# Late counts by prefix sums and minima, column forms with a second tensor, columns in a group's fifth block, and another order at start and end, in a one-core graph layer

## The chip, the cores and the metric

The kernel runs on one core of one Trainium2 chip. The metric is the device time of the kernel in microseconds (us); less is better. Engines are called PE (TensorE), DVE (VectorE), ACT (ScalarE), POOL (GpSimd) and SP (SyncE).

## The reference, cut to what matters

There are 50,000 nodes with 128 features and 1,650,000 edges, sorted by their target node. Every edge has a type, 0 or 1.

```python
m_data = X[src] @ W_data.T + b_data
m_ctrl = X[src] @ W_control.T + b_control
msg = where(edge_types == 0, m_data, m_ctrl)
agg = segment_sum(msg, dst, num_segments=50000)
out = relu(agg + X @ W_self.T + b_self)
return layernorm(x + out)
```

The weights are linear, so the kernel sums the source rows first, for each target node and type, and multiplies by the weights afterwards.

## The kernel before

**Blocks.** The edges are cut in order into 514 blocks (`NBLK`, numbers 0 to 513). A block's targets lie in a window of 112 nodes. A block holds `Q` = 2 steps of `R` = 12 chunks of 128 edges, so 24 chunks. POOL fetches the 128 source rows of a chunk (512 bytes each) by one indirect DMA, a *gather* (`gathers`, L536). Six gathers make a pass (`PASS`), a pass fills one buffer `y`, and there are ten buffers (`SLOTS`). PE multiplies each chunk's rows with a one-hot matrix of the chunk's target columns (128 x 120, both types side by side) and sums them in `acc` (`products`, L555). DVE builds the one-hot matrices of a whole block in one comparison (`onehot`, L467) and counts edges for the biases (`counts`, L475), two blocks ahead. `add` (L569) adds a step's sums to the block's.

**Single rows and fillers.** Besides its 24 chunks a block has 48 edges whose rows SP and ACT fetch one by one (`single_rows`, L510), and edges that fill the places which edges from a node to itself leave free in the chunks, since these are taken from the block's own rows. Such *fillers* come from a list per step with `F` = 46 places and `LATE` = 10 more for those that had to wait, `FX` = 56 in all. `spread(b)` (L347) is three small PE products that copy the list of block b to all partitions. `fill(b)` (L356 to L377) is DVE work: it finds which place takes which filler, writes the list `idx` of block b that the gathers read (L369) and the columns that `onehot` reads (L370). Blocks 0 and 513 are plain, without fillers; POOL needs no `fill` for them.

**Columns.** Ten blocks make a group (`GB`), 52 in all. `columns(g)` (L279 to L335) does for a whole group what can be done at once: the columns of its edges (`columns_of`, L240 to L243), checks (L248 to L251), the packed number of source and column (`packed`, L256 and L258), the list's three parts `v_f` (L296 to L302), the column numbers `cb` (L305 to L307), the rank of every free place (`rank` on PE, L284 and L286; `rk`, L311), and the number of waiting fillers `late`. That last is a chain: each of 20 steps is max(0, more + late of the step before), one `tensor_scalar` on a 128 x 1 column each (L323), as the group before left its last count.

**Order.** The order of all work is written out by hand, and each engine runs its instructions in that order. Before the loop stand the constants, the numbers of blocks (L207 to L223: windows, registers' values and shifts, needed by `window`, `positions` and the final checks), then the lines that make block 0, 1 and 2. The loop over b puts, in turn: spreads of the lists to be made, `add` of the block before, `onehot` and `counts` of block b+2, and four passes, between which stand `fill`, `layer(b-1)` (L586 to L590, the weights), `moments` (L596 to L603), `columns`, `store` (L618, L621: the normalised rows of a pair of blocks) and `store_rows` (L626, an output DMA per block on SP). Lists are made up to five blocks ahead (`RAHEAD`), two per block until then. `columns(g+1)` stands after the third pass of a group's second block:

```python
if q == 2 and i == 1 and g + 1 < GROUPS:
    columns(g + 1)
```

`find_bad` (L631 to L659) is a check of the input's form that chooses, at the end, whether the general version must run; it does not run here. It stands before the last block.

Of the kernel before, what the change touches and what calls it, by code (L numbers as in the profile page):

```python
# [12 lines left out]
F32 = mybir.dt.float32  # L13
BF16 = mybir.dt.bfloat16
# [9 lines left out]
N = 50000  # L24
# [57 lines left out]
GS = GB * Q  # L82
SPAN = 8
# [14 lines left out]
def straight(ctx, tc, c, x, x_t, edges_t, edges_f, src_x, dst_first, first_p, out):  # L98
# [62 lines left out]
    row_of = keep.tile([GB, GB], BF16, name="row_of")  # L161
    nc.vector.tensor_copy(row_of, c["ident"][:GB, :GB])
# [41 lines left out]
    nc.vector.tensor_tensor(begin_p, begin_p, base_p, op=ALU.add)  # L204
    wide = keep.tile([1, WG, SPAN], F32, name="wide")
    bases_f = keep.tile([1, WG * SPAN], F32, name="bases_f")
    nc.vector.memset(bases_f, float(N - B))  # L207
    nc.vector.tensor_copy(bases_f[:, :NBLK], base[0:1, :NBLK, 0])
    first_of_span = bases_f.rearrange("o (w s) -> o w s", s=SPAN)
    nc.vector.tensor_scalar(wide, first_of_span[:, :, 0:1].to_broadcast([1, WG, SPAN]), float(N - WIDE), None, op0=ALU.min)  # L210
    within = keep.tile([1, WG, SPAN], F32, name="within")
    nc.vector.tensor_tensor(within, first_of_span, wide, op=ALU.subtract)
    at_i = keep.tile([1, WG * SPAN, 4], I32, name="at_i")
    nc.vector.tensor_copy(at_i[:, :NBLK, :Q], begin[0:1, :NBLK, :])
    nc.vector.tensor_scalar(at_i[:, :, 3], within.rearrange("o w s -> o (w s)"), 0.0, float(WIDE - B), op0=ALU.max, op1=ALU.min)
    nc.vector.tensor_tensor(begin, begin, base.to_broadcast([P, BL, Q]), op=ALU.add)
    base_i = keep.tile([1, WG, 2 * SPAN], I32, name="base_i")
    nc.vector.tensor_scalar(base_i[:, :, 0], wide[:, :, 0], 4.0, None, op0=ALU.mult)
    nc.vector.tensor_scalar(base_i[:, :, 1:1 + SPAN], first_of_span, float(ROW), None, op0=ALU.mult)
    shift = keep.tile([1, NBLK], F32, name="shift")  # L220
    nc.vector.memset(shift, 0.0)
    nc.vector.tensor_tensor(shift[:, 1:], base[0:1, 1:NBLK, 0], base[0:1, :NBLK - 1, 0], op=ALU.subtract)
    nc.vector.tensor_scalar(at_i[:, :NBLK, 2], shift, 0.0, float(B), op0=ALU.max, op1=ALU.min)  # L223


# [10 lines left out]
    def columns_of(d, t, first, name):  # L236

        rel = eds.tile(list(d.shape), F32, name="rel" + name, bufs=1)
# [5 lines left out]
        return col, rel  # L244
# [8 lines left out]
    def packed(src, col):  # L253

        lim = eds.tile(list(col.shape), F32, name="lim", bufs=1)
        nc.vector.tensor_scalar(lim, col, 0.0, float(COLS - 1), op0=ALU.max, op1=ALU.min)  # L256
        v = eds.tile(list(col.shape), F32, name="v")
        nc.vector.scalar_tensor_tensor(v, src, float(COLS), lim, op0=ALU.mult, op1=ALU.add)  # L258
        return v

    def columns(g):
# [27 lines left out]
        col, rel = columns_of(a["d"], a["t"], first_of, "")  # L289
        check(a["d"], rel, [stats[:, 0, m, g:g + 1] for m in range(2)], "")  # L290
        col_f, rel_f = columns_of(a["df"], a["tf"], first_of_f, "_f")
# [5 lines left out]
        with nc.allow_low_precision(reason="whole numbers below 256 times a power of two"):  # L297
            nc.vector.tensor_scalar(v_f[:, 0, :], col_f, 0.0, float(COLS - 1), op0=ALU.max, op1=ALU.min)
            lo = eds.tile([GB, Q * FX], F32, name="lo", bufs=1)
            nc.vector.scalar_tensor_tensor(lo, hi, -float(COLS), a["sf"], op0=ALU.mult, op1=ALU.add)  # L300
# [14 lines left out]
        more = eds.tile([P, GS], F32, name="more", bufs=1)  # L315
        nc.vector.tensor_scalar(more, rank[:, :, R], -1.0, float(F), op0=ALU.mult, op1=ALU.add)
        late = eds.tile([P, GS + 1], F32, name="late")
        if g == 0:
            nc.vector.memset(late, 0.0)
        else:  # L320
            nc.vector.tensor_copy(late[:, 0:1], late_g[g - 1][:, GS:])
        for k in range(at, n):
            nc.vector.tensor_scalar(late[:, k + 1:k + 2], more[:, k:k + 1], late[:, k:k + 1], 0.0,  # L323
                                    op0=ALU.add, op1=ALU.max)
# [5 lines left out]
        if n < GS and g > 0:  # L330
            nc.vector.memset(late[:, n + 1:], 0.0)
# [8 lines left out]
    def spread(b):  # L340

        if plain(b):
            return
        g, i = divmod(b, GB)
        vf = lists[b % 2][:, :Q * FX]
        for m in range(3):
            nc.tensor.matmul(vf, row_of[:, i:i + 1].to_broadcast([GB, P]), vp_g[g][:, m, :], start=m == 0, stop=m == 2)  # L347
# [74 lines left out]
    def passes_of(b):  # L422

        for p in range(C // PASS):
            q = p * PASS // R
            yield q, [k for k in chunks_of(b, q) if k // PASS == p]
# [155 lines left out]
    def layer(b):  # L582
        a = sums[b % RING]
# [3 lines left out]
        nc.tensor.matmul(po, xT, c["wselfT"], start=True, stop=False)  # L587
        nc.tensor.matmul(po, a[0:3, 2, :B], bias, start=False, stop=False)  # L588
        for t in range(2):
            nc.tensor.matmul(po, a[:, t, :B], c["wmsgT"][:, t * D:(t + 1) * D], start=False, stop=t == 1)  # L590
        pos[b] = both

    def moments(b):
# [6 lines left out]
        if b % 2 == 0:  # L600
            mvs[b // 2] = stp.tile([B, 2, 2], F32, name="mv")
        mv = mvs[b // 2][:, b % 2, :]
        nc.vector.bn_aggr(mv, st)  # L603
        hs[b] = h

    def pair(b):

        return range(b // 2 * 2, b + 1) if b % 2 == 1 or b == NBLK - 1 else ()

    def root(bs):  # L610
        sd = stp.tile([B, 2], F32, name="sd")
        nc.scalar.activation(sd[:, :len(bs)], mvs[bs[0] // 2][:, :len(bs), 1], AF.Sqrt, bias=c["eps"][:B, :])
        sds[bs[0] // 2] = sd

    def store(bs):
        mv = mvs.pop(bs[0] // 2)
        rstd = stp.tile([B, 2], F32, name="rstd")
        nc.vector.reciprocal(rstd[:, :len(bs)], sds.pop(bs[0] // 2)[:, :len(bs)])  # L618
# [41 lines left out]

    for b in range(1, AHEAD + 1):
        offsets(b)
    columns(0)
    window(0)
    spread(1)
    fill(1)
# [3 lines left out]
    onehot(0)  # L670
    counts(0)
# [10 lines left out]
    for b in range(NBLK + 1):  # L682
        if b == NBLK - 1:
            find_bad()
# [5 lines left out]
        due, fresh = fresh, range(made + 1, min(b + RAHEAD, made + 2, NBLK - 1) + 1)  # L690
# [5 lines left out]
        if b < NBLK:  # L696
            begin_sums(b)
# [5 lines left out]
        for q, (step, ks) in enumerate(passes_of(b)):  # L703
# [21 lines left out]
            if q == 2 and i == 1 and g + 1 < GROUPS:  # L725
                columns(g + 1)
# [9 lines left out]
    store(pair(NBLK - 1))  # L736
    for b in (*ready, *pair(NBLK - 1)):
        store_rows(b)
# [338 lines left out]
```

## Time and profile before

| what | value |
|---|---|
| median of 3 runs | 17994.12 us (17983.56 to 17994.94) |
| profiled execution, its own time | 18008.86 us |
| its span | 18006.8 us |
| granted TensorE clock | 0.540 |
| POOL busy | 11686.9 us (65%) |
| DVE busy | 12374.8 us (69%) |
| PE busy | 8608.7 us (48%) |

In rows of groups the columns are: line, engine, operation, written tile <- read tiles, shapes, count; then busy time and the mean ns of one; then idle time of the engine just before them, and what ended it. Rows of waits give engine, tile and line, the releaser, the total, the number of times and the longest. Rows of the timeline give start, duration, engine, line, operation, and in brackets the idle time before with its releaser. "remote" is a releaser that the profile could not name, "issue" is time in which nothing visible was waited for.

### The profile page before, as it was taken

How to read it: one execution, taken by the hardware profiler on the slowest of the kernel's cores; microseconds unless marked ns; L12 is line 12 of the kernel's file. 1: busy time of each engine (PE TensorE's matmuls, PEld its weight loads, DVE VectorE, ACT ScalarE, POOL GpSimd, SP SyncE). 2: the span in 40 equal slices, each digit the busy share in tenths (PEclk: the TensorE clock that was granted, in tenths of full speed). 3: DMA queues.
4: the chain of work that ended last, by engine and by line, in shares of the span. 5: the costliest groups of instructions: out<-in, count | busy, mean ns of one | idle time of the engine just before them, and what ended most of it. 6: DMA issues, size and time to landing. Idle time of an engine off the chain costs nothing.

```text
span 18006.8 us, 165600 instructions
## 1 busy us (share of the span) xinstructions
PE 8608.7 (48%) x37659; PEld 7345.2 (41%) x37660; DVE 12374.8 (69%) x15212; ACT 79.2 (0%) x263; POOL 11686.9 (65%) x12341
## 2 busy tenths in 40 slices
PE   3444444444444444444444444444444444444444
PEld 3344443444344444444444444444444444444444
DVE  7676676676666666666766766676676676667665
ACT  0000000000000000000000000000000000000000
POOL 6666666666666666666666666666666666666666
PEclk6555555555555555555555555555555555555555
DMA  1111111111111111111111111111111111111111
GB/s 52 51 50 51 52 50 51 52 50 51 50 52 51 50 52 50 51 51 51 51 50 52 51 50 51 51 51 51 51 51 50 51 52 50 51 52 50 51 50 48
DMA packets 529272, 913.91 MB, mean 51 GB/s; under 512 B 232762, under 2 KB 315875, under 8 KB 528274
## 3 DMA queue, kind: packets, MB, share of 16 engines
q0 software_dynamic: 394592, 808.89, 15.7%
q1 hardware_dynamic: 108668, 87.80, 1.7%
q10 hardware_dynamic: 25014, 6.54, 0.2%
q8 instruction: 306, 5.01, 0.1%
q14 instruction: 692, 5.67, 0.1%
HBM read 872.82 MB, written 29.47 MB: 50 GB/s over the span
## 4 chain that ended last, share of the span: by engine, by line
DVE 51%; another core or an unknown queue 28%; issue 13%; PE 7%; DVEq 0%; ACTq 0%; ACT 0%
DVE cnt L475 14%; DVE oh L467 8%; PE acc L555 5%; DVE m L358 4%; DVE v_new L365 4%; DVE new L361 4%; DVE old L374 4%; DVE sums L569 2%; DVE late L323 1%; DVE z L392 1%; DVE h L597 1%; DVE st L599 1%; DVE xT L461 1%; DVE h L596 1%
## 5 line engine op out<-in xcount | busy, mean ns | idle before, releaser
L536 POOL DMA_INDIRECT y<-in_x,idx x12312 | 11667.4, 948 | 6272.6 <-issue 3435.2
L555 PEld LDWEIGHTS acc<-oh,y 128*128 128x128 f32 x24662 | 5375.0, 315 | 8665.3 <-issue 8100.0
L555 PE MATMUL acc<-oh,y 128*128 128x120 f32 x24662 | 6002.7, 413 | 3679.8 <-issue 3675.4
L569 DVE TENSOR_TENSOR sums<-acc,sums 128x180 f32 x1028 | 350.0, 340 | 4142.8 <-remote 3960.0
L475 DVE TENSOR_REDUCE cnt<-oh 128x240 bf16<-128x3120 f32 x514 | 3008.2, 5852 | 17.9
L384 PE MATMUL small<-ones_b,by 128*112 128x1 bf16 x512 | 83.5, 164 | 4632.6 <-issue 3934.5
L467 DVE TENSOR_TENSOR oh<-col,small 128x3120 f32<-128x3120 f32 x514 | 1740.8, 3387 | 117.3 <-remote 95.1
L377 DVE TENSOR_REDUCE by<-old 128x112 bf16<-128x1456 f32 x512 | 1427.3, 2788 | 17.4
L358 DVE TENSOR_TENSOR m<-rk,small 128x1456 f32<-128x1456 f32 x512 | 855.7, 1671 | 17.4
L361 DVE TENSOR_TENSOR new<-m,small 128x1456 f32<-128x1456 f32 x512 | 855.2, 1670 | 17.5
L365 DVE TENSOR_REDUCE v_new<-new 128x26 f32<-128x1456 f32 x512 | 855.0, 1670 | 17.5
L374 DVE TENSOR_TENSOR old<-m,small 128x1456 f32<-128x1456 f32 x512 | 852.5, 1665 | 0.0
L561 PE MATMUL acc<-oh,yx 24*128 24x120 f32 x2048 | 758.6, 466 | 61.6 <-issue 61.6
L590 PE MATMUL po<-wmsgT,sums 128*112 128x128 f32 x2056 | 612.8, 453 | 5.5 <-issue 5.5
L561 PEld LDWEIGHTS acc<-oh,yx 24*128 24x128 f32 x2048 | 486.9, 292 | 293.0 <-issue 281.7
L596 DVE COPY h<-po 112x128 f32<-112x128 f32 x514 | 144.8, 282 | 537.1 <-remote 451.3
L590 PEld LDWEIGHTS po<-wmsgT,sums 128*112 128x112 f32 x2056 | 448.4, 297 | 130.7 <-issue 130.0
L347 PE MATMUL small<-v_f,row_of 10*128 10x112 bf16 x1536 | 218.2, 272 | 563.8 <-DVE at L391 168.6
L588 PE MATMUL po<-bias,sums 3*112 3x128 f32 x1028 | 391.5, 482 | 0.2 <-DVE sums L569 0.2
L347 PEld LDWEIGHTS <-row_of 10*128 10x128 bf16 x1536 | 121.7, 112 | 599.5 <-issue 562.2
L587 PE MATMUL po<-wselfT,xT 128*112 128x128 f32 x1028 | 324.9, 420 | 0.0
L564 PE MATMUL acc<-cnt,to_row 128*128 128x60 bf16 x2056 | 281.2, 227 | 13.8 <-issue 13.7
(141 smaller groups left out, 4709.2 us busy)
## 6 DMA issues: line engine op xcount, KB each, us to landing
y<-in_x,idx POOLq DMA_INDIRECT x12312
yx<-in_x SPq DMA_DIRECT2D x12288, 0.5 KB
yx<-in_x ACTq DMA_DIRECT2D x12288, 0.5 KB
xw<-in_x_t SPq DMA_DIRECT2D x65, 448.0 KB
out<-o SPq DMA_DIRECT2D x514, 56.0 KB
sdt<-in_edges_t SPq DMA_DIRECT2D x52, 390.0 KB
one_g<-in_src_x SPq DMA_DIRECT2D x52, 1.9 KB
sdt_f<-in_edges_f SPq DMA_DIRECT2D x52, 13.1 KB
```

Source lines behind the costliest of these rows:

```text
L358: nc.vector.tensor_tensor(m, rk_g[g][:, i, :, None].to_broadcast([P, C1, FX]), rank_no_ps[:, None, :].to_broadcast([P, C1, FX]), op=ALU.is ...
L361: nc.vector.tensor_tensor(new.rearrange("p (q r) f -> p q r f", r=R1), m.rearrange("p (q r) f -> p q r f", r=R1), vf.rearrange("p (q f) -> ...
L365: nc.vector.tensor_reduce(v, new, AX.X, ALU.add)
L374: nc.vector.tensor_tensor(old, m, cb[:, :, None].to_broadcast([P, C1, FX]), op=ALU.mult)
L377: nc.vector.tensor_reduce(by, old.rearrange("p (q r) f -> p q f r", r=R1), AX.X, ALU.add)
L467: nc.vector.tensor_tensor(oh, col_g[g][:, i, :, None].to_broadcast([P, C1, 2 * W]), num_ps[:, None, :].to_broadcast([P, C1, 2 * W]), op=AL ...
L475: nc.vector.tensor_reduce(cnt, ohs[b].rearrange("p (q r) w -> p q w r", r=R1), AX.X, ALU.add)
L536: copy = nc.gpsimd.indirect_dma_start(out=y[:r, k % PASS, :].bitcast(U8), out_offset=None, in_=x_rows, in_offset=bass.IndirectOffsetOnAxis ...
L555: nc.tensor.matmul(acc[:, :2, :].rearrange("p t w -> p (t w)"), y[:r, k % PASS, :], ohs[b][:r, column(k), :], start=k == of_step[0], stop= ...
L561: nc.tensor.matmul(acc[:, :2, :].rearrange("p t w -> p (t w)"), ys[b][:, q, :], ohs[b][:S, q * R1 + R, :], start=False, stop=True)
L569: nc.vector.tensor_tensor(part, accs.pop((b, q)), part, op=ALU.add)
L590: nc.tensor.matmul(po, a[:, t, :B], c["wmsgT"][:, t * D:(t + 1) * D], start=False, stop=t == 1)
```

## The change

It touches five places.

1. The chain of late counts becomes sums and minima over shifted copies: with prefix sums `total` of the steps' balances and the running minimum `least` of these, late = total - least. A tile `runs` of two pairs of lines, with 16 zeros (`PAD`) ahead of each, holds them; five additions and five minima at shifts 1, 2, 4, 8 and 16, and one subtraction.
2. Operations with one tensor and constants in `columns` become `scalar_tensor_tensor` with a second tensor: a new `nz` for types, `lim`, and the parts of `v_f`. `nz` is used by `col` and `cb`, so `cb` has one operation fewer, and `lo` goes. `row_of` gets a second plane.
3. The numbers of blocks become a function `block_numbers`, called after `fill(1)`; `columns(0)` comes first.
4. The first blocks make one list per block, two only from block 6 on, and `columns(g+1)` goes from a group's second to its fifth block.
5. At the end `find_bad` moves one block earlier; the last block has passes of two chunks; block 512 gets its layer and its store before the products of block 513, and 513 is stored alone, by `together` and `pair`.

```diff
+    ones_f = keep.tile([P, 1], F32, name="ones_f")
+    runs = keep.tile([P, 4, PAD + GS + 1], F32, name="runs")
+    nc.vector.memset(runs, 0.0)
...
+    row_of = keep.tile([GB, 2, GB], BF16, name="row_of")
+    nc.vector.tensor_copy(row_of[:, 0, :], c["ident"][:GB, :GB])
+    nc.vector.tensor_scalar(row_of[:, 1, :], c["ident"][:GB, :GB], float(COLS), None, op0=ALU.mult)
...
+    def block_numbers():
+        nc.vector.memset(bases_f, float(N - B))
...
+        nc.vector.tensor_scalar(at_i[:, :NBLK, 2], shift, 0.0, float(B), op0=ALU.max, op1=ALU.min)
...
+        nc.vector.scalar_tensor_tensor(nz, t, 0.0, one.to_broadcast(list(d.shape)), op0=ALU.not_equal, op1=ALU.mult)
...
-        nc.vector.tensor_scalar(col, t, 0.0, float(W), op0=ALU.not_equal, op1=ALU.mult)
-        nc.vector.tensor_tensor(col, col, rel, op=ALU.add)
+        nc.vector.scalar_tensor_tensor(col, nz, float(W), rel, op0=ALU.mult, op1=ALU.add)
...
-        nc.vector.tensor_scalar(lim, col, 0.0, float(COLS - 1), op0=ALU.max, op1=ALU.min)
+        nc.vector.scalar_tensor_tensor(lim, col, 0.0, last_f[:, :, None].to_broadcast(list(col.shape)),
+                                       op0=ALU.max, op1=ALU.min)
...
-            nc.vector.tensor_scalar(v_f[:, 1, :], lo, float(COLS), None, op0=ALU.mult)
-            nc.vector.tensor_scalar(v_f[:, 2, :], hi, float(COLS * COLS), None, op0=ALU.mult)
+            nc.vector.scalar_tensor_tensor(v_f[:, 1, :], hi, -float(COLS), a["sf"], op0=ALU.mult, op1=ALU.add)
+            nc.vector.scalar_tensor_tensor(v_f[:, 2, :], v_f[:, 1, :], -1.0, a["sf"], op0=ALU.mult, op1=ALU.add)
...
-        nc.vector.tensor_scalar(cb, a["t"], 0.0, float(P), op0=ALU.not_equal, op1=ALU.mult)
-        nc.vector.tensor_tensor(cb, cb, a["d"], op=ALU.add)
+        nc.vector.scalar_tensor_tensor(cb, nz, float(P), a["d"], op0=ALU.mult, op1=ALU.add)
...
+        by, i = 1, 0
+        while by <= GS:
+            nc.vector.tensor_tensor(up[:, 1 - i, PAD:], up[:, i, PAD:], up[:, i, PAD - by:PAD + GS + 1 - by], op=ALU.add)
+            by, i = 2 * by, 1 - i
+        total = up[:, i, PAD:]
+        least, by, i = up[:, i, :], 1, 0
+        while by <= GS:
+            nc.vector.tensor_tensor(low[:, i, PAD:], least[:, PAD:], least[:, PAD - by:PAD + GS + 1 - by], op=ALU.min)
+            least, by, i = low[:, i, :], 2 * by, 1 - i
...
-        for k in range(at, n):
-            nc.vector.tensor_scalar(late[:, k + 1:k + 2], more[:, k:k + 1], late[:, k:k + 1], 0.0,
-                                    op0=ALU.add, op1=ALU.max)
+        nc.vector.tensor_tensor(late, total, least[:, PAD:], op=ALU.subtract)
...
+        of = 2 if b == NBLK - 1 else PASS
...
+    def together(b):
+
+        return range(b, b + 1) if b == NBLK - 1 else range(b // 2 * 2, min(b // 2 * 2 + 2, NBLK - 1))
...
+    columns(0)
+    spread(1)
+    fill(1)
+    block_numbers()
     for b in range(1, AHEAD + 1):
         offsets(b)
-    columns(0)
     window(0)
-    spread(1)
-    fill(1)
+    onehot(0)
+    counts(0)
     left_out_columns(1)
     left_out_matrix(1)
     positions(0)
-    onehot(0)
-    counts(0)
     clear_sums()
...
-    for b in range(NBLK + 1):
+    for b in range(NBLK):
+        if b == NBLK - 2:
+            find_bad()
         if b == NBLK - 1:
-            find_bad()
+            if pair(b - 2):
+                store(pair(b - 2))
+                ready.extend(pair(b - 2))
+            while ready:
+                store_rows(ready.pop(0))
...
-        due, fresh = fresh, range(made + 1, min(b + RAHEAD, made + 2, NBLK - 1) + 1)
+        due, fresh = fresh, range(made + 1, min(b + RAHEAD, made + (2 if b > GB // 2 else 1), NBLK - 1) + 1)
...
+        if b == NBLK - 1:
+            layer(b - 1)
+            moments(b - 1)
+            root(pair(b - 1))
+            own_part(b)
+            store(pair(b - 1))
+            for done in pair(b - 1):
+                store_rows(done)
+            for step, ks in passes_of(b):
...
+            break
...
-            if q == 2 and i == 1 and g + 1 < GROUPS:
+            if q == 2 and i == GB // 2 - 1 and g + 1 < GROUPS:
                 columns(g + 1)
...
-    store(pair(NBLK - 1))
-    for b in (*ready, *pair(NBLK - 1)):
-        store_rows(b)
+    b = NBLK - 1
+    add(b, steps_of(b)[-1])
+    layer(b)
+    moments(b)
+    root(pair(b))
+    store(pair(b))
+    store_rows(b)
```

More of the change, by code (lines that the diff above doesn't have):

```diff
@@ L82 @@
 GS = GB * Q
+PAD = 16
 SPAN = 8
@@ L204, in straight @@
     nc.vector.tensor_tensor(begin_p, begin_p, base_p, op=ALU.add)
+    nc.vector.tensor_tensor(begin, begin, base.to_broadcast([P, BL, Q]), op=ALU.add)
     wide = keep.tile([1, WG, SPAN], F32, name="wide")
     bases_f = keep.tile([1, WG * SPAN], F32, name="bases_f")
-    nc.vector.memset(bases_f, float(N - B))
-    nc.vector.tensor_copy(bases_f[:, :NBLK], base[0:1, :NBLK, 0])
     first_of_span = bases_f.rearrange("o (w s) -> o w s", s=SPAN)
-    nc.vector.tensor_scalar(wide, first_of_span[:, :, 0:1].to_broadcast([1, WG, SPAN]), float(N - WIDE), None, op0=ALU.min)
@@ L346, in spread @@
         for m in range(3):
-            nc.tensor.matmul(vf, row_of[:, i:i + 1].to_broadcast([GB, P]), vp_g[g][:, m, :], start=m == 0, stop=m == 2)
+            nc.tensor.matmul(vf, row_of[:, min(m, 1), i:i + 1].to_broadcast([GB, P]), vp_g[g][:, m, :], start=m == 0, stop=m == 2)
     def fill(b):
@@ L580, in begin_sums, with own_part @@
             nc.vector.tensor_tensor(part, pls.pop(b)[:, :, :B], old, op=ALU.add)
-    def layer(b):
-        a = sums[b % RING]
+    def own_part(b):
         both = ps_o.tile([B, 2, D], F32, name="po")
@@ L587, in layer @@
         nc.tensor.matmul(po, xT, c["wselfT"], start=True, stop=False)
+        pos[b] = both
+    def layer(b):
+        if b not in pos:
+            own_part(b)
+        a = sums[b % RING]
+        po = pos[b][:, 0, :]
         nc.tensor.matmul(po, a[0:3, 2, :B], bias, start=False, stop=False)
```

86 lines of the change are left out of this document (47 added, 39 removed).

## The prediction

> **What bounds the kernel now.** I read the page's busy times first, then the waits, then the gathers as a group, and last single gathers in the timeline.
>
> ```profile
> span 18006.8 us, 165600 instructions
> PE 8608.7 (48%) x37659; PEld 7345.2 (41%) x37660; DVE 12374.8 (69%) x15212; ACT 79.2 (0%) x263; POOL 11686.9 (65%) x12341
> DVE sums L569 <- remote: 3960.0, 513, 20.4
> POOL y L536 <- remote: 2192.3, 743, 6.7
> L536 POOL DMA_INDIRECT y<-in_x,idx x12000 | 11370.0, 948 | 6110.1 <-issue 3346.7 <-remote 2144.6 <-DVE old L374 214.7
> 363.68 0.94 POOL L536 DMA_INDIRECT y<-in_x,idx  x1 [3.98 <-remote]
> 9234.12 0.94 POOL L536 DMA_INDIRECT y<-in_x,idx  x1 [2.91 <-remote]
> 9251.85 0.94 POOL L536 DMA_INDIRECT y<-in_x,idx  x1 [2.64 <-remote]
> 9269.30 0.95 POOL L536 DMA_INDIRECT y<-in_x,idx  x1 [2.68 <-PE po L590]
> 17841.67 0.94 POOL L536 DMA_INDIRECT y<-in_x,idx  x1 [1.81 <-PE acc L555]
> ```
>
> No engine is full. The rows of gathers say how the three work together: 12000 gathers (the group's count) begin between 363.68 and 17841.67, so one takes 17477.99 / 12000 = 1.4565 us, 34.96 us per block, 349.6 us per group of ten blocks. POOL needs 0.948 us of work for each, and 3346.7 / 12000 = 0.28 us to issue it; the other 0.23 us is waiting for a buffer that TensorE has not yet emptied. The waits come regularly, once every twelve gathers or so: 9234.12, 9251.85 and 9269.30 are 17.73 and 17.45 us apart, where twelve gathers on the line make 17.48. VectorE meanwhile waits 3960.0 us, in 513 of the 514 blocks, for the sums. So the time is set by the ring gather, product, buffer free, and VectorE is not its limit as a rule. Three places can then be worth something: how late the line starts, what disturbs it once a group, and what follows its last gather.
>
> **The start.** Run back 240 gathers, the line at 363.68 begins at 363.68 - 240 x 1.4565 = 14.1 us.
>
> ```profile
> 3.03 1.15 POOL L536 DMA_INDIRECT y<-in_x,idx  x1 [0.91 <-DMA idx<-in_edges_t]
> 33.80 0.95 POOL L536 DMA_INDIRECT y<-in_x,idx  x1 [0.30 <-issue]
> 46.20 0.95 POOL L536 DMA_INDIRECT y<-in_x,idx  x1 [11.45 <-DVE idx L369]
> 162.76 1.12 POOL L536 DMA_INDIRECT y<-in_x,idx  x1 [5.17 <-PE acc L555]
> 12.66 0.49 DVE L207 MEMSET bases_f<- 1x520 f32 x1
> 16.16 1.21 DVE L216 TENSOR_TENSOR begin<-begin,base 128x1040 f32<-128x1040 f32 x1
> 20.09 0.28 DVE L279 MEMSET h_loop<- 128x260 bf16 x1
> 27.29 0.46 DVE L323 TENSOR_SCALAR late<-more,late 128x1 f32<-128x1 f32 x2
> 39.31 0.17 DVE L327 TENSOR_REDUCE most<-late 128x1 f32<-128x18 f32 x1
> 40.20 0.18 DVE L356 COPY small<-cb 128x26 f32<-128x26 f32 x1
> 45.75 0.18 DVE L369 TENSOR_SCALAR idx<-vi 128x26 int32<-128x26 int32 x1
> 52.09 3.40 DVE L467 TENSOR_TENSOR oh<-col,small 128x3120 f32<-128x3120 f32 x1
> 61.39 0.62 DVE L232 MEMSET sums<- 128x672 f32 x1
> 65.43 0.16 DVE L356 COPY small<-cb 128x26 f32<-128x26 f32 x1
> L367 DVE TENSOR_TENSOR vi<-v_new,stay 128x26 int32<-128x26 f32 x512 | 95.6, 187 | 17.5
> ```
>
> The first gather began at 3.03, so the start costs 14.1 - 3.0 = 11.1 us. About 8 of it are the wait of 11.45 us for the list of block 1 (46.20 - 24 x 1.4565 = 11.2, against 3.0); some 3 more come by the wait of 5.17 at 162.76, in a block 1 that holds two fills and the next group's columns.
>
> What the change moves here: the block numbers go behind fill(1). From 12.66 to 20.09 VectorE spent 7.4 us, of which only L216 (1.2) stays; columns(0) then starts near 13.9. The chain of late counts took 27.29 to 39.31, 12.0 us for 18 steps; now it is 12 short operations (one for the missing, five additions, five minima, one difference) at the 0.187 us of the nearest two-input row, L367: 2.3 us. The list needs 20.09 to 27.29 (7.2), 2.3, then 0.9 to the copy at 40.20 and 5.7 to the end of idx: 13.9 + 7.2 + 2.3 + 0.9 + 5.7 = 30.0, before POOL asks at 35.05 (33.80 + 1.25). If the new steps are delayed as the old ones were (12.0 / 18 = 0.67 each, 8.0 us), the list comes at 35.7 and POOL waits 0.7. The stall goes in either case.
>
> What is late next is the list of block 2, asked for at 35.05 + 24 x 1.25 = 65.1 (0.95 of work and 0.30 of issue each); before it was 46.20 + 30.0 = 76.2. VectorE's order after idx at 30.0: rest of fill(1) and left-out work 6.2 (45.93 to 52.09), block numbers 6.2, one-hot and counts 9.3 (52.09 to 61.39), clearing 4.0 (61.39 to 65.43), list 5.7: 61.4, 3.7 us in time. With the eleven moved steps at the old chain's pace of 0.67 it is 62 to 63, at twice that 70, and POOL waits 5. After that lists are made one per block until block 5, so each is just in time, where before POOL had two in hand. TensorE starts on block 0 some 11 us earlier, as one-hot and counts end near 50 instead of 61.4. The gain lies between all 11 and nothing, or a loss of about as much if several early lists are late; I take -6: the first stall gone, half of it paid again on the lists of blocks 2 to 8.
>
> **Once a group.** Here the late chain shrinks, tensor_scalar becomes a form with a second tensor, and the columns go from the second to the fifth block of a group.
>
> ```profile
> 9241.62 1.10 POOL L536 DMA_INDIRECT y<-in_x,idx  x1 [0.31 <-issue]
> 9248.11 1.10 POOL L536 DMA_INDIRECT y<-in_x,idx  x1 [0.30 <-issue]
> 26.30 0.95 POOL L536 DMA_INDIRECT y<-in_x,idx  x1 [0.31 <-issue]
> 26.37 0.43 DVE L307 TENSOR_TENSOR cb<-cb,before 128x260 f32<-128x260 f32 x1
> 9240.12 0.28 DVE L279 MEMSET h_loop<- 128x260 bf16 x1
> 9252.33 4.96 DVE L323 TENSOR_SCALAR late<-more,late 128x1 f32<-128x1 f32 x20
> 9257.87 0.43 DVE L335 SCALAR_TENSOR_TENSOR stay<-rk,v 128x260 f32<-128x260 f32 x1
> 9262.54 0.16 PE L384 MATMUL small<-ones_b,by 128*112 128x1 bf16 x1 [9.97 <-DVE oh L467]
> 9262.64 2.92 PE L555 MATMUL acc<-oh,y 128*128 128x120 f32 x12
> L256 DVE TENSOR_SCALAR lim<-col 128x260 f32<-128x260 f32 x52 | 14.4, 277 | 0.0
> L258 DVE SCALAR_TENSOR_TENSOR v<-sdt,lim 128x260 f32<-128x260 int32 x52 | 22.3, 430 | 7.6 <-remote 4.2 <-DVE lim L256 1.7
> ```
>
> The columns hold VectorE from 9240.12 to 9258.30, 18.2 us. The chain's 4.96 become 2.3; three wide forms grow by 0.430 - 0.277 = 0.15 each and one wide operation of 0.28 goes: 2.5 us less VectorE. But POOL's releases at 9234.12, 9251.85 and 9269.30 run straight past this work, so its worth is nothing while TensorE's pass at 9262.64, which waited until 9262.54 behind VectorE, ends (9265.56) before the release at 9269.30: a cover of 3.7 us. What the columns do cost on the line are the lengthened gathers beside them, 1.10 instead of 0.95 at 9241.62 and 9248.11, 0.30 us a group, 51 x 0.30 = 15 us. By the row at 26.30 a gather beside a whole operation with two tensors stays at 0.95, so the new forms would give all 15 back; but at 9241.62 the gather lies beside such operations too and took 1.10. Bounds -15 and 0 (+15 if the longer operations hold it longer); I take -8.
>
> The Trainium skill, page "SBUF — State Buffer", section "Who interferes with whom", says that tensor_scalar and copies can enter a mode that takes a port pair exclusively, with GpSimd fully blocked, and that an operation with two SBUF inputs contends only with a GpSimd operation's reads. The row at 26.30 agrees, that at 9241.62 does not fit it alone; by the rule the term would be the whole -15.
>
> **The end.** Find_bad moves a block earlier, the last block goes in passes of two chunks, block 512 is stored before the products of 513.
>
> ```profile
> 17946.03 0.95 POOL L536 DMA_INDIRECT y<-in_x,sdt  x1 [3.88 <-PE acc L564]
> 17981.63 0.19 PE L651 MATMUL po<-ones,bad 128*3 128x1 f32 x2
> 17984.10 5.45 PE L555 MATMUL acc<-oh,y 128*128 128x120 f32 x24
> 17992.91 8.37 SPq L626 DMA_DIRECT2D out<-o  x4
> ```
>
> From the last block's first gather to the span's end pass 18006.8 - 17946.03 = 60.8 us. Taken away: the 2.5 us that TensorE stood behind find_bad (17981.63 to 17984.10), and one store of the chain of four, whose four last from 17992.91 for 8.37 us, some 2.8 from one to the next; now one is issued after the last output instead of two. Given back: the passes of block 512 stand behind find_bad instead, and 513's 24 products (5.45 us from 17984.10) stand behind 512's layer, whose sums VectorE must first finish. Ten short passes also take ten buffers where four took four, so the last block's last gathers wait for the products of block 512; those were through before 17981.63, early enough that 513's need not end later than now. Bounds -6 and +2; I take -3, since the store is at the very end and the rest is exchanged.
>
> **Sum.** -6 - 8 - 3 = -17 us. The profiled execution took 18008.86 (its span 18006.8 and 2 around it), 15 above the median 17994.1; it would be 17992, the median 17977. A measurement of this kernel can tell about 0.2%, 36 us.
>
> **Rivals.** *Columns are on the path.* Waits named "remote" hide who released, and at 162.76 POOL stood 5.17 us in a block with columns. If 1 us of the 2.5 that columns become shorter comes back each group, 51 more us go: 17926; all of it would be 17850. Against it speak the straight releases at 9234 to 9269. It decides if the slack of 3.7 us is used up in many groups.
>
> *Columns too close to their first list (slower).* The first list of the next group is spread by TensorE at the start of the sixth block, and that matmul waits for values that columns makes in the fifth, with the block's passes queued behind it on TensorE. Before, there were four blocks between. If columns (18.2 us) run into it by more than the cover of 3.7 us, say by 5.2, POOL waits 1.5 us longer each group: 51 x 1.5 = 77, less the 17: 18054. For it: at 9262.54 TensorE had already stood 9.97 us behind VectorE after columns. Against: the values needed come in columns' first half, before the one-hot for which TensorE waits anyway.
>
> *Nothing arrives.* The stall of 11.45 is replaced by late lists in blocks 2 to 8, the lengthened gathers stay, the end exchanges one wait for another: 17991.
>
> **How the numbers follow.** Forecast 0.52, its own range 17960 to 18005: below, all three lower bounds together (17994 - 32 = 17962); above, an early loss of 11, nothing from the columns, and the end as taken (18002); columns on the path 0.26; columns too close 0.14; nothing arrives 0.08. Faster by over 0.2% (below 17958) are the second case and 0.04 of the first's tail, with every bound reached and the longer operations giving back a little more: 0.30. Slower by over 0.2% (above 18030) is the third: 0.14. The rest, 0.56, lies within. The range 17920 to 18010 leaves out the slower case and 0.06 of the faster one.
>
> **What the changed profile would show.** Right: POOL's 25th gather near 35, no wait of some 11 us for idx; the line's start near 8 instead of 14.1; 349.3 to 349.6 us per group, gathers beside columns back at 0.95; 58 us from the last block's first gather to the end. Wrong: waits of POOL for idx in blocks 2 to 8 that add to more than 6 us; a pitch below 349 per group (columns were on the path); or POOL waiting over 4 us once a group beside the first list of the next.

## The result, and the profile after

| kernel | median of 20 runs | lowest to highest |
|---|---|---|
| before | 17984.58 us | 17975.90 to 17995.46 |
| changed | 17956.59 us | 17953.68 to 17963.09 |

The ratio of changed to before is 0.9985, 95% interval 0.9979 to 0.9991: 28 us between the medians, about 0.16%. The forecast was 17 us less. The time lies in the stated range, 17920 to 18010 us, and the difference is within 0.2%. The profiled execution of the changed kernel took 17956.11 us, its span 17954.0. That is 52.8 us less than the first span of before, 18006.8. By the medians, then, nearly half of what the two profiles differ by is not the change; the first question is which half.

Gathers are numbered from 0 here, so the 240th has 240 ahead of it and is the first of block 10, and the 12312th is the first of the last block. The page of the changed kernel, its waits of VectorE and POOL, and its gathers from the 240th on as one group:

```profile
span 17954.0 us, 165064 instructions
PE 8584.6 (48%) x37659; PEld 7319.4 (41%) x37660; DVE 12266.2 (68%) x14661; ACT 79.5 (0%) x264; POOL 11657.6 (65%) x12341
DVE sums L588 <- remote: 3704.4, 496, 18.1
POOL y L555 <- remote: 2312.4, 778, 4.9
L555 POOL DMA_INDIRECT y<-in_x,idx x12072 | 11409.5, 945 | 6147.9 <-issue 3340.7 <-remote 2278.3 <-PE acc L574 178.6
```

The picture is that of before: VectorE waits 496 times for the sums, and POOL waits some 2300 us for buffers. VectorE has 109 us less work (12374.8 to 12266.2), far more than the time became shorter.

The timeline of the changed kernel, at the places that bound the three stretches:

```profile
3.06 1.15 POOL L555 DMA_INDIRECT y<-in_x,idx  x1 [0.95 <-DMA idx<-in_edges_t]
31.16 0.18 DVE L387 TENSOR_SCALAR idx<-vi 128x26 int32<-128x26 int32 x1
56.76 0.24 DVE L244 MEMSET sums<- 3x224 f32 x1 [1.63 <-issue]
69.72 0.18 DVE L387 TENSOR_SCALAR idx<-vi 128x26 int32<-128x26 int32 x1
70.92 0.94 POOL L555 DMA_INDIRECT y<-in_x,idx  x1 [6.42 <-DVE idx L387]
351.04 0.94 POOL L555 DMA_INDIRECT y<-in_x,idx  x1 [2.99 <-remote]
17909.38 0.94 POOL L555 DMA_INDIRECT y<-in_x,sdt  x1 [3.89 <-remote]
```

The 240th gather starts at 351.04 instead of 363.68: 12.6 us. The last block's first gather, the 12312th, starts 17558.34 us later; that is 349.07 us per 240 gathers, where before had 349.55 (17946.03 - 363.68 over 12072 gathers): 24 us over the whole stretch. From there to the end of the span pass 44.6 us instead of 60.8: 16 us. Together 52.8. The middle term, the time per 240 gathers or *pitch*, is the one that the experiments had to judge.

### The profile page after: what moved, and what is told of

Read it like the earlier page. It is cut to its first block, busy times and chain, and to the rows that moved or that the text cites. A ratio compares the mean times of both kernels' runs of the same rounds, so it can differ in the third digit from the quotient of the medians.

```text
span 17954.0 us, 165064 instructions
## 1 busy us (share of the span) xinstructions
PE 8584.6 (48%) x37659; PEld 7319.4 (41%) x37660; DVE 12266.2 (68%) x14661; ACT 79.5 (0%) x264; POOL 11657.6 (65%) x12341
## 4 chain that ended last, share of the span: by engine, by line
DVE 48%; another core or an unknown queue 27%; issue 15%; PE 10%; DVEq 0%; SPq 0%; DMA 0%; ACT 0%; ACTq 0%
DVE cnt L494 13%; DVE oh L486 7%; PE acc L574 7%; DVE m L376 4%; DVE v_new L383 4%; DVE new L379 4%; DVE old L392 4%; DVE sums L588 1%; DVE z L410 1%; DVE h L621 1%; DVE st L623 1%; PE acc L580 1%; PE po L615 1%; DVE xT L480 1%
## 5 line engine op out<-in xcount | busy, mean ns | idle before, releaser
L300 PEld LDWEIGHTS <-ones_b 128*128 128x128 bf16 x624 | 78.7, 149 | 671.3 <-issue 659.8
```

## The experiments

A comparison here is always with the kernel before in the same group of runs on the same chip, since the runs came to several chips, on which that kernel's median was 17883.5, 17881.1, 15467.6 and 18018.2 us. The table gives medians against it, and from each profile the three stretches.

| run | against before | 240th gather | us per 240 gathers | last stretch |
|---|---|---|---|---|
| b_again | -2.2 | 357.2 | 347.05 | 58.4 |
| a_end | -13.7 | 352.6 | 347.07 | 58.4 |
| a_order | -20.0 | 354.0 | 347.19 | 43.4 |
| a_chain | -21.9 | 349.0 | 347.18 | 44.5 |
| a_again | -26.7 | 348.5 | 347.06 | 47.1 |
| a_of6 | -17.3 | 354.4 | 347.01 | 56.3 |
| a_cols | -27.9 | 349.2 | 346.96 | 53.0 |
| a_forms | -26.8 | 348.2 | 347.07 | 47.1 |
| b_of2 | -0.6 | 321.6 | 300.25 | 39.6 |
| a_fill2 | -3.9 | 304.6 | 300.61 | 36.6 |
| a_sub3 | -5.8 | 304.6 | 300.57 | 36.7 |
| a_best | +3.2 | 351.0 | 350.21 | 50.2 |

The first four rows are one group, the next four the second, then three, then one. Every ratio in these groups has an interval of about plus or minus 0.0009, 16 us; the medians of 11 runs are steadier than that (b_again, the same kernel twice, differs by 2.2 us), and the stretches of the profiles say where a difference lies. Differences below some 5 us are not told from none. A single stretch of a single profile is less steady than a median: profiles with the changed end and passes of two have a last stretch of 43.4 to 53.0 us where POOL waits for buffers, so the end is judged by medians.

**The kernel before again (b_again).** No edit.

> The kernel before, unchanged, profiled again beside the others. Theory A (the ends): the 28 us between the medians are made at the start (line of gathers begins at 1.4 instead of 14.3 us) and behind the last block's first gather (44.6 instead of 60.8 us); the pitch of the two kernels is the same, and the 0.45 us a group by which the two profiles differ (349.55 and 349.11) is a pace of the chip or execution, seen in gathers that wait for nothing (1.2512 and 1.2484 us apart). So here: about 349.1 us per group, start near 14.3, last stretch near 60. Theory B (the groups): shorter columns in another block take 0.45 us off each group, 23 us in all; then 349.5 us per group here, and the two ends together are worth some 5 us in the median.

And **the changed kernel again (a_again)**, in the next group:

> The changed kernel, unchanged, profiled again beside the kernel before and the next three. Theory A (the ends) expects the chip's pitch for both, start between 1 and 5 us, last stretch 44 to 45 us, and 20 to 28 us less than the kernel before. Theory B (the groups) expects a pitch about 0.45 us a group below that of the kernel before run again.

Gathers as a group, and the ends of the stretch, first of b_again and then of a_again:

```profile
L536 POOL DMA_INDIRECT y<-in_x,idx x12072 | 11439.5, 948 | 6018.3 <-issue 3357.5 <-remote 2113.8 <-PE acc L555 162.3
357.17 0.95 POOL L536 DMA_INDIRECT y<-in_x,idx  x1 [3.88 <-PE acc L555]
17813.88 0.95 POOL L536 DMA_INDIRECT y<-in_x,sdt  x1 [2.82 <-remote]
```

```profile
L555 POOL DMA_INDIRECT y<-in_x,idx x12072 | 11439.1, 948 | 6017.5 <-issue 3347.5 <-remote 2112.5 <-PE acc L574 163.2
348.51 0.94 POOL L555 DMA_INDIRECT y<-in_x,idx  x1 [2.99 <-remote]
17805.85 0.95 POOL L555 DMA_INDIRECT y<-in_x,sdt  x1 [3.73 <-remote]
```

The two groups agree row for row: 11439 us of work, 6018 us of idleness, 347.05 and 347.06 us per 240 gathers. These two ran on different chips, but a_end below, which has the new columns too, ran on b_again's chip and has 347.07. The pitch is no part of the change, theory A is right. Theory B falls, and with it the 24 us between the first two profiles: the pitch differs between sets of runs (347 to 350 us here) and the first profile of before happened to have a slow one. What A said of the reason was wrong too: gathers that wait for nothing were 1.251 us apart in a_again and 1.248 in the first profile of the same kernel, but the pitch of the groups doesn't follow that.

**The old end (a_end).** find_bad before the last block, passes of six, both last blocks stored after the loop:

```diff
-        if b == NBLK - 2:
+        if b == NBLK - 1:
             find_bad()
...
-        of = 2 if b == NBLK - 1 else PASS
+        of = PASS
...
-            store(pair(b - 1))
-            for done in pair(b - 1):
-                store_rows(done)
...
+    store(pair(NBLK - 1))
+    for b in (*ready, *pair(NBLK - 1)):
+        store_rows(b)
```

> The changed kernel with the end of the kernel before (find_bad before the last block, passes of six there, blocks 512 and 513 in a pair, both stored after the loop). Theory A: the last stretch grows from 44.6 to about 60 us, 16 us slower than the changed kernel, near 17972. Theory B: 3 to 5 us slower, near 17961, since the long end of the first profile was that execution's.

13.7 us under before where the changed kernel is 26.7 under it: the new end is worth 13 us, and the last stretch is 58.4 again. Close to theory A's 16. The other 13.7 us belong, by elimination, to the start: against b_again, on the same chip, this run has the same pitch (347.07 and 347.05) and the same last stretch (58.4). Its profile's 240th gather is only 4.6 us earlier than b_again's, whose profiled execution, 17874.3 us, was 7 us faster than its median.

**Passes of six in the last block (a_of6).** One line of the new end:

```diff
-        of = 2 if b == NBLK - 1 else PASS
+        of = PASS
```

> The changed kernel with passes of six chunks in the last block instead of two; all else of the new end stays. Theory A1 (the long run of 19 gathers without a pause slows TensorE's steps, as in the profile of before between 17956 and 17973): the stretch from the last block's first gather to the end grows from 44.6 by some 7 us, to about 52. Theory A2 (the gain of the end is find_bad and the store): it grows by 1 to 2 us.

It is 9.4 us slower than a_again, the stretch 56.3 instead of 47.1 (that its profile's 240th gather is late as well has to do with the start, below). So most of the end's 13 us is in this line; find_bad, the stores and the new order of block 512 keep about 3.6 (17.3 against a_end's 13.7 under before). TensorE and POOL in the last stretch of a_of6, and then POOL's first pause in that of a_again:

```profile
17819.85 1.07 PE L615 MATMUL po<-wmsgT,sums 128*112 128x128 f32 x2 [1.65 <-issue]
17822.59 0.94 POOL L555 DMA_INDIRECT y<-in_x,sdt  x1 [0.30 <-issue]
17822.66 0.37 PE L615 MATMUL po<-wmsgT,sums 128*112 128x128 f32 x1 [1.74 <-issue]
17824.74 0.37 PE L615 MATMUL po<-wmsgT,sums 128*112 128x128 f32 x1 [1.72 <-issue]
17826.84 0.37 PE L421 MATMUL pl<-z,to_row 112*128 112x128 bf16 x2 [1.03 <-issue]
17827.01 5.42 PE L574 MATMUL acc<-oh,y 128*128 128x120 f32 x24
17827.13 0.95 POOL L555 DMA_INDIRECT y<-in_x,sdt  x1 [3.60 <-remote]
```

```profile
17817.55 0.94 POOL L555 DMA_INDIRECT y<-in_x,sdt  x1 [1.99 <-remote]
```

TensorE does one or two products at a time and then stands 1.0 to 1.7 us on "issue", beside POOL's gathers and on into POOL's pause. POOL pauses after the gather at 17822.59 (its next stands at 17827.13 with 3.60 us of waiting), and from 17827.01 TensorE runs 24 products in one stretch, beside POOL's next gathers. In a_again the last block's gathers pause after eight instead of twelve, and TensorE is through earlier. It is not that products waited for the six gathers of a pass: in a_of6 the last gather starts at 17834.63, and the last block's products at 17850.84.

The same shows all along the line, worked out from a_again's trace: TensorE's products stand on "issue" 3% of the time or less in the first 12 us after a pause of POOL (pauses over 1.5 us), 40% from 14 to 16 us after it, and 69 to 76% from 16 to 22 us. So a long run of gathers without a pause goes together with the standing, and making POOL wait earlier is the likely reason why small passes help. It is argued, not shown: a pause of POOL ends when TensorE frees a buffer, so the rows alone do not tell which of the two drives the other.

**Buffers of two alone (b_of2).** The kernel before, with this alone:

```diff
-        y = gathers(b, ks)
+        of = 2 if b == NBLK - 1 else PASS
         for k in ks:
+            if k % of == 0:
+                y = gathers(b, [j for j in ks if j // of == k // of])
```

> The kernel before with one part of the change alone: the chunks of the last block go through buffers of two instead of six, so POOL pauses between them; order, find_bad and stores stay as before. If the long run of gathers slows TensorE's steps (theory A1), the last stretch shrinks by 7 to 9 us, from 58 to about 50, as it grew by 9 when only this was undone. If the gain of the passes needs the new order of block 512 and 513, it stays within 2 us of the kernel before.

No gain, but on a chip where the question doesn't arise, as its rows below show. It decides nothing for the end where POOL waits, and the edit was not run there.

**The old start order (a_order).**

```diff
+    block_numbers()
+    for b in range(1, AHEAD + 1):
+        offsets(b)
     columns(0)
+    window(0)
     spread(1)
     fill(1)
-    block_numbers()
-    for b in range(1, AHEAD + 1):
-        offsets(b)
-    window(0)
-    onehot(0)
-    counts(0)
     left_out_columns(1)
     left_out_matrix(1)
     positions(0)
+    onehot(0)
+    counts(0)
```

> The changed kernel with the start order of before: block numbers ahead of columns(0), one-hot and counts of block 0 after the left-out work and positions; the short chain of late counts stays. Theory A: the list of block 1 comes some 7 us later, near 38, POOL waits about 3 us for it, the lists after it are late too; start between 5 and 9 instead of 1.4, 4 to 8 us slower. Theory B: the start is given back later, within 2 us of the changed kernel.

20.0 under before, 6.7 above the changed kernel by medians taken on two chips, each against its own kernel before; the 240th gather at 354.0 instead of 348.5. That fits theory A, but a profile with the unchanged start has 354.4 too (a_of6), so the first list's wait says more than the 240th gather. That wait is back, with the short chain in place, and longer than the 3 us expected; in a_chain below, with the old chain and the new order, it is nearly gone. The first gather of block 1 (24 gathers ahead of it) in a_order, then in a_chain:

```profile
44.92 0.94 POOL L555 DMA_INDIRECT y<-in_x,idx  x1 [10.61 <-DVE idx L387]
```

```profile
34.88 0.94 POOL L549 DMA_INDIRECT y<-in_x,idx  x1 [1.11 <-DVE idx L381]
```

So it is the order, not the short chain, that takes the first stall away.

**The serial chain (a_chain).**

```diff
+        for k in range(at, n):
+            nc.vector.tensor_scalar(late[:, k + 1:k + 2], more[:, k:k + 1], late[:, k:k + 1], 0.0,
+                                    op0=ALU.add, op1=ALU.max)
```

> The changed kernel with the serial chain of late counts of before (20 one-column steps per group). Theory A: costs only at the start, 3 us if the steps run at 0.25 us each, up to 9 if at 0.67; after that nothing, the pitch per group stays. Theory B: VectorE's 2.5 us per group are on the path in part; at a tenth of it 13 us, at all of it 128 us slower.

4.8 us slower than the changed kernel by the medians, at the limit of what can be told from none. Its start is that of the changed kernel (240th gather at 349.0 and 348.5), so these microseconds are not seen there; the pitch is 0.12 us per group more, which the other profiles scatter by too. The chain's group in a_chain, and the two groups in its place in the changed kernel:

```profile
L335 DVE TENSOR_SCALAR late<-more,late 128x1 f32<-128x1 f32 x1024 | 219.5, 214 | 36.3 <-DVE late L335 0.4
```

```profile
L336 DVE TENSOR_TENSOR runs<-runs 128x21 f32<-128x21 f32 x260 | 47.3, 182 | 9.0
L341 DVE TENSOR_TENSOR runs<-runs 128x21 f32<-128x21 f32 x260 | 47.5, 183 | 9.0
```

219.5 us of VectorE become 94.8 and one subtraction per group, at 0.18 us a step where 0.187 was forecast, and no more than a few us of it reach the end.

**Columns in the second block (a_cols).**

```diff
-            if q == 2 and i == GB // 2 - 1 and g + 1 < GROUPS:
+            if q == 2 and i == 1 and g + 1 < GROUPS:
```

> The changed kernel with columns(g+1) after the third pass of a group's second block, as before, instead of its fifth. Theory A: same pitch, within 0.1 us a group; with columns(1) in block 1, which also makes a list, the start of the line is 1 to 4 us later; 0 to 5 us slower. Theory B: the pitch rises by 0.2 to 0.45 us a group, 10 to 23 us slower. Third possibility, that the fifth block is the worse place: 3 to 10 us faster.

1.2 us faster than a_again, the pitch 0.10 us lower: no difference. The place of columns costs and brings nothing that these runs can tell. Its last stretch of 53.0, with an end that is the same as a_again's, is not explained by the edit.

**The one-tensor forms (a_forms).** For example:

```diff
-        nc.vector.scalar_tensor_tensor(lim, col, 0.0, last_f[:, :, None].to_broadcast(list(col.shape)),
-                                       op0=ALU.max, op1=ALU.min)
+        nc.vector.tensor_scalar(lim, col, 0.0, float(COLS - 1), op0=ALU.max, op1=ALU.min)
```

> The changed kernel with the one-tensor forms of before in columns (tensor_scalar for col, lim, the parts of v_f and cb; row_of's first plane alone is used). By the step of the prediction that put -8 us on gathers beside columns, their lengthening goes up again and the run is about 8 us slower. Theory A, since the profile after has no less lengthening (139 gathers, 22.9 us over the usual, against 196 and 21.2): within 3 us of the changed kernel.

17854.29 against 17854.44: none of the 8 us.

**The list of block 2 first (a_fill2).**

```diff
-    clear_sums()
     spread(2)
     fill(2)
+    clear_sums()
```

> The changed kernel with the list of block 2 made ahead of the clearing of the sums. The list of block 2 then comes 4 us earlier or more. If the wait for it (none, 6.4, 7.0, 10.9 and 12.3 us in five profiles of the same start) decides where the line of gathers begins, the slow starts go: line near 1 us, some 3 us less in the median. If TensorE's first products decide, which wait for the cleared sums, no change within 2 us.

What the start still varies by is seen in two profiles of identical starts. VectorE's list of block 2 in a_again, then three rows of a_of6:

```profile
61.86 0.18 DVE L387 TENSOR_SCALAR idx<-vi 128x26 int32<-128x26 int32 x1
```

```profile
48.05 0.68 DVE L235 TENSOR_TENSOR shift<-base 1x513 f32<-1x513 f32 x1 [3.47 <-remote]
76.55 0.18 DVE L387 TENSOR_SCALAR idx<-vi 128x26 int32<-128x26 int32 x1
77.00 0.94 POOL L555 DMA_INDIRECT y<-in_x,idx  x1 [12.34 <-DVE idx L387]
```

The list comes at 61.9 or at 76.6, after waits of VectorE whose cause the profile doesn't show ("remote" in the first of the three rows), and the 240th gather stands at 348.5 or 354.4. The other profiles answer in part what a_fill2 was to tell. Take the pitch off the 240th gather, and where POOL did not wait for block 2's list the line of gathers begins at 1.1 us (a_forms) and 1.4 (a_again); with a wait of 6.4 and 7.0 us at 2.0 and 2.2 (the first profile, a_cols); with 10.9 and 12.3 at 5.5 and 7.4 (a_end, a_of6). A wait of up to 7 us goes with a line about one microsecond later; what is longer than that comes back nearly in full. On the chip that a_fill2 came to, its start is no test: a_sub3, without this edit, doesn't wait for block 2's list there either and has the same 304.6.

**What that chip shows.** The chip of b_of2, a_fill2 and a_sub3 is called the quick chip from here on. Gathers of b_of2 and of a_fill2 as groups between 330 and 15400 us, with b_of2's two long waits at the start, and then TensorE's products in a_fill2 (PEq is TensorE's sequencer, at the wait for a gather's landing):

```profile
39.14 0.94 POOL L536 DMA_INDIRECT y<-in_x,idx  x1 [3.85 <-DVE idx L369]
149.24 0.94 POOL L536 DMA_INDIRECT y<-in_x,idx  x1 [13.05 <-PE acc L557]
L536 POOL DMA_INDIRECT y<-in_x,idx x12047 | 11398.3, 946 | 3673.1 <-issue 3671.5 <-PE acc L566 0.3 <-PE acc L557 0.3
```

```profile
L555 POOL DMA_INDIRECT y<-in_x,idx x12032 | 11402.5, 948 | 3668.2 <-issue 3666.1 <-PE acc L583 0.6 <-DVE old L392 0.3
L574 PE MATMUL acc<-oh,y 128*128 128x120 f32 x24662 | 5965.1, 432 | 6368.4 <-PEq L562 6368.0
```

Behind the start POOL waits for no buffer to speak of: 300 us a group is 240 gathers of 1.25 us. TensorE waits for gathers, not on "issue". Here every lengthened gather counts, and here the columns of the change cost something. Summed over the gathers beside columns, what each took beyond the usual 944 ns is 23.7 us in b_of2 and 43.7 us in a_fill2. At the start a_fill2 gains 17.0 us (321.6 to 304.6), at the end 3.0; the stretch between gives back 18.1 (15102.56 to 15120.67), nearly all that the gathers are longer by. Two gathers of a_fill2 beside the new forms of one group, then one of b_of2 beside an old form, a `tensor_scalar`:

```profile
7372.07 1.17 POOL L555 DMA_INDIRECT y<-in_x,idx  x1 [0.31 <-issue]
7373.55 1.29 POOL L555 DMA_INDIRECT y<-in_x,idx  x1 [0.30 <-issue]
7373.60 0.41 DVE L318 SCALAR_TENSOR_TENSOR cb<-nz,sdt 128x260 f32<-128x260 f32 x1
7374.04 0.43 DVE L319 TENSOR_TENSOR cb<-cb,before 128x260 f32<-128x260 f32 x1
```

```profile
7291.82 1.13 POOL L536 DMA_INDIRECT y<-in_x,idx  x1 [0.30 <-issue]
7292.55 0.28 DVE L305 TENSOR_SCALAR cb<-sdt 128x260 f32<-128x260 int32 x1
```

Both forms go together with longer gathers. Gathers that lie beside the whole of `cb<-nz,sdt` take 1.26 us on average in a_fill2 (44 gathers), those beside the whole of `cb<-sdt` 1.13 us in b_of2 (51 gathers); other operations lie beside the same gathers, so this doesn't price one operation.

**Buffers of three (a_sub3).**

```diff
-SLOTS = 10
+SLOTS = 20
+SUB = 3
...
         for k in ks:
+            if k % SUB == 0 or k == ks[0]:
+                y = gathers(b, [j for j in ks if j // SUB == k // SUB])
```

> The changed kernel with buffers of three chunks instead of six in every block, 20 of them instead of 10, the same memory. What is asked: does the finer release, which helped in the last block, move the pitch of all blocks? If POOL's waits of 2.5 us per twelve gathers come from the size of a buffer, the pitch falls by up to some 2%, 7 us a group, 350 us in all. If they come from TensorE's position, which is a fixed distance behind, it stays within 1 us a group, and the last block loses some of its gain because 20 buffers let its gathers run through.

On this chip there is no wait to shorten; 1.9 us under a_fill2, which is not told from none.

**The three together (a_best).** Buffers of three, the list of block 2 first, the one-tensor forms.

> The changed kernel with three edits that cost nothing so far: buffers of three chunks (20 of them), the list of block 2 ahead of the clearing, and the one-tensor forms of before in columns. Where gathers run without waiting (pitch 300 us a group, as in the last three runs): the changed kernel's columns there lengthened gathers by 43 us in all, the kernel before by 24. If the second tensor does it, about 24 again and 15 to 20 us less than the 15462 to 15464 of the last two; if columns' place or the short chain of late counts does it, 42 to 44 and the same time as those. Where POOL waits for buffers twice a block (pitch 347 us): 17 to 28 us under the kernel before if the finer buffers leave the pitch alone, some hundred us if they shorten the waits of 2.5 us.

It came to a chip where POOL waits, and is no faster than the kernel before: 18021.4 and 18018.2 us, ratio 1.0001 (0.9992 to 1.0010). Its gathers between the same marks:

```profile
L555 POOL DMA_INDIRECT y<-in_x,idx x12072 | 11407.6, 945 | 6210.0 <-issue 3235.8 <-remote 1491.1 <-PEq L562 519.5
```

Idleness between gathers is 6210 us, and 6148 in the first profile of the changed kernel on another chip: there is no sign that the waits became shorter. Since its start (351.0) and end (50.2) look like the changed kernel's, the loss must lie in the pitch of 350.21; the kernel before was not profiled on that chip, so this is argued, not shown, and which of the three edits costs it is open. The changed kernel itself was not run there. Where it was, and POOL waits, no other version was clearly faster.

## Why the prediction was right, and where it wasn't

**What bounds the kernel** held: where POOL waits for buffers, the ring of gather, product and free buffer sets the pitch, and VectorE's work on the columns is worth nothing that can be measured beside it. What the ring's slow part is, TensorE standing on "issue", the prediction didn't see; on the quick chip that part is gone, and the line is POOL's alone. a_chain gives VectorE over 110 us of work back for 4.8 us, a_cols and a_forms move nothing. The rival that columns are on the path (0.26) is refuted by these, and the slower rival, columns too close to their first list, by a_again and a_cols, which have the same pitch. "Nothing arrives" is refuted by the 28 us.

**The start** was the right mechanism at half its size. -6 was taken; a_end against its kernel before gives 13.7 by the medians, and the profiles give 8.7 us (357.2 to 348.5 in b_again and a_again, on two chips) and 12.6 (the first two). Block 1's list came at 31.2 (forecast 30.0), in time. Block 2's came at 69.7 in the first profile, 61.9 in a_again (forecast 61.4), with a wait of 6.4 or none (forecast: up to 5), and of 12.3 in a_of6. What was wrong was to charge such a wait to the line in full: with 6.4 us of it the 240th gather still stood at 351.0, 12.6 earlier than before, and the line began at 2.0 where "near 8" was forecast. By the prediction's own sign, waits for the lists of blocks 2 to 8 of more than 6 us, the first profile would have spoken against it; the sign was badly chosen. That TensorE's earlier beginning lets the line start sooner in spite of the wait is likely, but no run here shows it.

**Once a group** is the step that failed. -8 was taken for gathers no longer lengthened beside columns. The extra time of gathers beside columns, over each profile's usual gather of 944 or 947 ns, is 19.0 us in the first profile of before and 21.6 in that of the change, 20.4 and 20.2 in b_again and a_again: nothing went. And where POOL waits for buffers anyway, a lengthened gather costs nothing that the pitch shows, as the prediction's own reading of the pitch should have said: it priced them as if the line were POOL's. Where POOL doesn't wait they do cost, and there the sign was the other: 20 us more. The prediction gave half its weight to the row of the gather at 26.30, not lengthened beside an operation with two tensors; the gather at 9241.62 was the better witness, and so are the gathers of 1.17 and 1.29 us in a_fill2. That agrees with one half of what the Trainium skill says on the page "SBUF — State Buffer", section "Who interferes with whom", that a VectorE operation with two SBUF inputs contends with a GpSimd operation that reads SBUF. What the prediction drew from the half about the exclusive mode, a term of -15, is not borne out here: in a_forms, which has these operations back, the gathers beside columns took 21.4 us extra, in a_again 20.2. Whether the second tensor alone makes the 20 us is open: a_best with the old forms was to tell, and came to a chip where POOL waits (17.3 us beside columns there).

**The end** was mis-sized: -3 against 13 us by the medians and 16 in the first two profiles. Find_bad and the store were counted, and come to about the size that was forecast, 3.6 us (a_of6 against a_end). The passes of two were put among the costs ("ten buffers where four took four, so the last block's last gathers wait") and priced at nothing. They are the gain: 9.4 of the 13 us go when the passes are six again. That the wait itself brings it is the likely reading, as said above.

**Sum.** -6, -8 and -3 stand against about -13.7, 0 and -13; these add up to a_again's 26.7 by the way they were taken, and of the parts undone one at a time only the order (6.7 us) and the passes (9.4) lie above what can't be told from none. The total came nearer than its terms, since one was too large and two too small; that is luck, not a right sum. The measured time, 17956.6, lies 20 us below the forecast median of 17977 and just below the 17960 to 18005 given to that case; 9.5 of the 20 are the kernel before, whose median was 17984.6 this time instead of 17994.1. The prediction's base, a profile 24 us above the median of its kernel, did no harm because the difference was taken from the median; as a basis for comparing pitches it was bad.

## What to carry to other kernels

Before a difference of two profiles is explained, run the old kernel again beside the new one: a pitch that differs by 0.13% need not be the change's. Price an operation's side effect by what bounds the stretch it lies in; here lengthened gathers cost nothing measurable where POOL waits for buffers (a_forms), and nearly all they were longer by where it doesn't (18.1 of 20 us). At the end of a kernel a queue that can run far ahead need not be let to: here smaller passes, which hold it back, were worth 9.4 us.

## What the runs showed of the hardware that was not expected

The kernel before took 17881 us on one chip and 15468 on another, at a lower granted TensorE clock (0.508 in a_fill2 on the quick chip, 0.542 in a_again). What differs in the profiles is whether TensorE stands on "issue" between its products, as in a_of6. Its products in the first profile of the kernel before; the row of a_fill2 above is the other side:

```profile
L555 PE MATMUL acc<-oh,y 128*128 128x120 f32 x24662 | 6002.7, 413 | 3679.8 <-issue 3675.4
```

3675 us here, none on the quick chip, with the same 24662 products. What makes a chip, or a set of runs, the one or the other is not shown by any run here. On the quick chip this change, with block 2's list made first, was 3.9 us under the kernel before, which is not told from none; on two others it was worth some 27.
